# A two-layer graph network: load order, product order and sum order at the start of its first aggregation

## The chip, the cores and the metric

The kernel runs on one core of a Trainium2 chip. The metric is the device time of one execution in microseconds (us); the number quoted for a kernel is the median of its executions.

## The reference, cut to what matters

There are 16 graphs `x` of 1024 nodes with 128 features, and one adjacency matrix of 1024 x 1024 for all of them, everything in fp32.

```python
def _layernorm(x, axis=-1, eps=1e-5):
    m = jnp.mean(x, axis=axis, keepdims=True)
    v = jnp.var(x, axis=axis, keepdims=True)
    return (x - m) / jnp.sqrt(v + eps)

# layer 0
support = jnp.einsum('bnf,fo->bno', x, weight)
output = jnp.einsum('nm,bmo->bno', adj, support) + bias
x = _layernorm(x + output)

# layer 1: five steps of a gated unit
def step(h, _):
    m_in = jnp.einsum('nm,bmd->bnd', in_matrix, h)     # both matrices are adj
    m_out = jnp.einsum('nm,bmd->bnd', out_matrix, h)
    av = jnp.concatenate([m_in, m_out], axis=-1)
    u3 = h @ u3_w.T + u3_b
    z = jax.nn.sigmoid(av @ w3_w.T + w3_b + u3)
    r = jax.nn.sigmoid(av @ w4_w.T + w4_b + u3)
    hv = jnp.tanh(av @ w5_w.T + w5_b + (r * h @ u5_w.T + u5_b))
    return ((1.0 - z) * h + z * hv, None)
x = _layernorm(x + scan(step, x, length=5))
```

The costly part is adjacency times features: once per graph in layer 0, five times in layer 1. The kernel handles four graphs at a time, so there are four such aggregations in layer 0 and twenty in layer 1. The change bears on the first of these twenty-four alone.

## The kernel before

One aggregation multiplies the adjacency by the features of four graphs with Strassen's scheme (Winograd's form), on two levels. The outer level makes seven products from 2 x 2 blocks; they are done in four groups, the chains `(1, 2)`, `(3,)`, `(6, 7)` and `(5, 4)`. Within a chain, each outer product is made of seven inner ones, P1 to P7. The sums and differences of blocks that this needs run on VectorE. P1 and P2 take blocks as they are; the other five need a sum on at least one side or come later in the chain.

For the very first aggregation the adjacency has to be loaded in eight pieces (`c` = 0 to 7, 128 rows each) and turned by TensorE, and the left sums have to be made. They are then kept for all the others.

The loads and the tiles:

```python
    queues = (nc.sync, nc.scalar)

    adj_rows = adj.rearrange("(h p n c) m -> n h p c m", h=2, n=4, c=2)
    raws = [agg[:, c] if c < CH else hid[:, c - CH] for c in range(C)]   # C = 8, CH = 4
    for h in range(2):
        for c in range(h * CH, h * CH + CH):
            queues[c % 2].dma_start(raws[c], adj_rows[c // 2, c % 2])
        for k in (2 * h, 2 * h + 1):
            queues[k % 2].dma_start(rows[:, k], x_rows(k))
    # ... cut ...
    blk = [const.tile([P, 2, CH, HALF], F32, name=f"a{i}") for i in range(2)]
    # ... s1, s2, s4: [P, CH, HALF] ...
    outer = {
        1: blk[0][:, 0], 2: blk[0][:, 1], 3: s4, 4: blk[1][:, 1], 5: s1, 6: s2, 7: blk[1][:, 0],
    }
```

The left sums and the turns. `bank` gives one of three PSUM banks in turn, and the copy out of it is done by VectorE for the first half of pieces 0 to 3 and by ScalarE for the rest:

```python
    def left_sums(a11, a12, a21, a22, s1, s2, s3, s4):
        nc.vector.tensor_add(s1, a21, a22)
        nc.vector.tensor_sub(s2, s1, a11)
        nc.vector.tensor_sub(s4, a12, s2)
        return nc.vector.tensor_sub(s3, a11, a21)

    def inner_left(n):
        lt = left[n]
        left_sums(lt[1], lt[2], quarter(n, 1, 0), lt[4], lt[5], lt[6], lt[7], lt[3])
    # inner_left_12: the same for outer products 1 and 2 at once, into e12

    def turn_adj(c):
        cols = raws[c].rearrange("p (q k) -> p k q", k=C)
        i, at = divmod(c, CH)
        for j in range(2):
            pt = bank(f"pt_adj_{c}_{j}")
            pt3 = pt.rearrange("p (k q) -> p k q", k=CH)
            for k in range(CH):
                nc.tensor.transpose(pt3[:, k, :], cols[:, j * CH + k, :], ident)
            dst = blk[i][:, j, :, ts(at, P)]
            if j == 0 and i == 0:
                nc.vector.tensor_copy(dst, pt3)
            else:
                nc.scalar.copy(dst, pt3)

    for t in (pb, *seeded):            # seeding products: 12 of 128 columns
        for k in range(CH):
            nc.tensor.matmul(t[:, ts(k, P)], ident, ident, start=(k == 0), stop=True,
                             skip_group_check=True)
    for c in range(CH):
        turn_adj(c)
    last_left = inner_left_12()
```

One chain: the bank of P1 (`pa`) is copied into `pb` as the base of P6, P7 and P4, and `pc` collects P5 and P3. `hooks` names work that is put ahead of a product.

```python
    def chain(tag, src, turned, ns, results, hooks, order=(1, 5, 6, 2, 7, 3, 4)):
        # ... cut: xs, right, flat ...
        pa = ps_m.tile([P, HALF], F32, tag="a", name=f"pa_{tag}")
        pc = ps_m.tile([P, HALF], F32, tag="c", name=f"pc_{tag}")
        fa, fb, fc = flat(pa), flat(pb), flat(pc)
        x11, x12, x21, x22 = results(0, 0), results(0, 1), results(1, 0), results(1, 1)
        after = {
            1: lambda: nc.scalar.copy(fb, fa),
            5: lambda: nc.scalar.copy(x22, fc),
            6: lambda: nc.scalar.copy(x12, fb),
            2: lambda: nc.scalar.copy(x11, fa),
            7: lambda: nc.vector.tensor_add(x22, fb, x22),
            3: lambda: nc.vector.tensor_add(x12, fc, x12),
            4: lambda: nc.scalar.copy(x21, fb),
        }
        bank_of = {1: pa, 2: pa, 5: pc, 3: pc, 6: pb, 7: pb, 4: pb}
        for a in order:
            for hook in hooks.get(a, ()):
                hook()
            for o, n in enumerate(ns):
                for c in range(2):
                    product = nc.tensor.matmul(
                        bank_of[a][:, ts(o, QT)], chunk(a, o, c), left[n][a][:, c, :],
                        start=(a in (1, 5) and o == 0 and c == 0), stop=(c == 1),
                        skip_group_check=True,
                    )
            # ... cut ...
            with tc.high_priority(), behind:
                after[a]()
```

So a product is four instructions in a chain of two outer products and two in the chain `(3,)`. The first aggregation is set up like this:

```python
    def turn_rest():
        for c in range(CH, C):
            turn_adj(c)

    def outer_left():
        left_sums(outer[1], outer[2], outer[7], outer[4], s1, s2, outer[7], s4)
        inner_left(3)
    # ... in the loop over groups of four graphs ...
        if q == 0:
            hooks[12] = {
                5: [turn_rest],
                6: [outer_left, call(sums_of, rows, (3,))],
                7: [call(outer_sums, rows), call(inner_left, 6), call(inner_left, 7)],
            }
            hooks[67] = {1: [call(inner_left, 5), call(inner_left, 4)]}
            layer0_weights()
            with tc.issue_after(last_left.ins):
                sums_of(rows, (1, 2))
```

The second aggregation takes along the projections (by the layer's weight) of the first one's four graphs, with their layer normalisations. ScalarE puts the bias into a PSUM bank, TensorE adds eight products of 128 columns, VectorE adds `x` and takes the statistics, GpSimd makes scale and shift, and ScalarE applies them:

```python
    def project(q, k, y):
        # ... cut ...
        for h in range(2):
            po = seeded[h]
            with tc.high_priority():
                tc.keep_in_program_order(nc.scalar.copy(po3, b0_bc...))
            for c in range(CH):
                nc.tensor.matmul(po3[:, c, :], chunk_cols(agg[:, k], h * CH + c), w0_sb, ...)
            with tc.high_priority():
                nc.vector.tensor_add(y[:, ts(h, CH), :], po3, y[:, ts(h, CH), :])
        layernorm(y, f"0_{b}", chunked(saved[b]))

    # in layernorm
        nc.gpsimd.tensor_scalar(rstd, mv[:, :, 1], EPS, None, ALU.add)
        nc.gpsimd.tensor_tensor(rstd, rstd, power[:, :n], ALU.pow)
        nc.gpsimd.tensor_tensor(shift, mv[:, :, 0], rstd, ALU.mult)
        nc.gpsimd.tensor_scalar(shift, shift, -1.0, None, ALU.mult)
        # ... and for each of eight parts
            nc.scalar.activation(y[:, c, :], y[:, c, :], AF.Identity,
                                 bias=shift[:, c : c + 1], scale=rstd[:, c : c + 1])
```

What no call pins is put in order by the framework's scheduler when the kernel is built; after that each engine's list is fixed.

Of the kernel before, what the change touches and what calls it, by code (L numbers as in the profile page):

```python
# [10 lines left out]
F32 = mybir.dt.float32  # L11
# [9 lines left out]
def kernel(  # L21
# [99 lines left out]
    for h in range(2):  # L121
        for c in range(h * CH, h * CH + CH):
            queues[c % 2].dma_start(raws[c], adj_rows[c // 2, c % 2])
        for k in (2 * h, 2 * h + 1):
            queues[k % 2].dma_start(rows[:, k], x_rows(k))
# [28 lines left out]

    def left_sums(a11, a12, a21, a22, s1, s2, s3, s4):
        nc.vector.tensor_add(s1, a21, a22)
        nc.vector.tensor_sub(s2, s1, a11)
        nc.vector.tensor_sub(s4, a12, s2)
        return nc.vector.tensor_sub(s3, a11, a21)
# [5 lines left out]
    def inner_left_12():  # L165
        a = [[blk[0][:, :, 2 * j : 2 * j + 2, ts(i, QT)] for j in range(2)] for i in range(2)]
        return left_sums(*a[0], *a[1], e12[:, :, 0], e12[:, :, 1], e12[:, :, 3], e12[:, :, 2])

    def turn_adj(c):
        cols = raws[c].rearrange("p (q k) -> p k q", k=C)  # L170
# [4 lines that stand above are left out]
            for k in range(CH):  # L175
                nc.tensor.transpose(pt3[:, k, :], cols[:, j * CH + k, :], ident)
            dst = blk[i][:, j, :, ts(at, P)]
            if j == 0 and i == 0:
                nc.vector.tensor_copy(dst, pt3)
            else:  # L180
                nc.scalar.copy(dst, pt3)


    for t in (pb, *seeded):
        for k in range(CH):
            nc.tensor.matmul(t[:, ts(k, P)], ident, ident, start=(k == 0), stop=True,
                             skip_group_check=True)
    for c in range(CH):
        turn_adj(c)
    last_left = inner_left_12()  # L190


# [6 lines left out]
    power = const.tile([P, C], F32, name="power")  # L199
    nc.vector.memset(power, -0.5)  # L200
# [105 lines left out]
    def sums_of(src, ns, pinned=False):  # L306
        t = inner[0 if ns in ((1, 2), (6, 7)) else 1]
        for op in inner_sums(blocks_of(src, ns), [t[:, i, : len(ns)] for i in range(4)]):
            if pinned:
                tc.keep_in_program_order(op)  # L310
        return op
# [4 lines left out]
    def outer_sums(src, early=True, late=True):  # L316

        lo, hi = src[:, 0:2], src[:, 2:4]
        if early:
            nc.vector.tensor_sub(tsum[:, 2], hi[:, :, HALF:], hi[:, :, :HALF])  # L320
            nc.vector.tensor_add(tsum[:, 1], tsum[:, 2], lo[:, :, :HALF])
        if late:
            nc.vector.tensor_sub(tsum[:, 0], hi[:, :, :HALF], lo[:, :, :HALF])
            return nc.vector.tensor_sub(tsum[:, 3], lo[:, :, HALF:], tsum[:, 1])  # L324

    def chain(tag, src, turned, ns, results, hooks, order=(1, 5, 6, 2, 7, 3, 4)):
# [31 lines left out]
        bank_of = {1: pa, 2: pa, 5: pc, 3: pc, 6: pb, 7: pb, 4: pb}  # L358
        for a in order:
            for hook in hooks.get(a, ()):  # L360
                hook()
# [7 lines that stand above are left out]

                    if turned and a in (5, 6, 2) and ns in ((1, 2), (3,)) and o == c == 0:  # L370
                        tc.keep_in_program_order(product)

            behind = tc.issue_after(closed[0].ins) if closed[0] else nullcontext()
            with tc.high_priority(), behind:
                after[a]()
# [4 lines left out]
    def aggregate(tag, src, hooks, turned=True):  # L380

        c12 = agg[:, 2:4, :HALF]
# [9 lines left out]
        chain(f"12_{tag}", src, turned, (1, 2), into(first), hooks.get(12, {}))  # L392
# [6 lines left out]
        with tc.issue_after(last_outer.ins) if turned else nullcontext():  # L399
            chain(  # L400
                f"3_{tag}", src, turned, (3,), lambda i, k: agg[:, 2 + k : 3 + k, ts(i, QT)],
                hooks.get(3, {}),
# [3 lines left out]
        chain(f"67_{tag}", src, turned, (6, 7), into(src[:, 0:2]), hooks.get(67, {}))  # L406
# [5 lines left out]
            order=(1, 5, 6, 2, 7, 4, 3),  # L412
# [201 lines left out]
    def turn_rest():  # L614
        for c in range(CH, C):
            turn_adj(c)

    def outer_left():
        left_sums(outer[1], outer[2], outer[7], outer[4], s1, s2, outer[7], s4)
        inner_left(3)  # L620

    for q in range(NQ):
        room = rooms[q % 2]
        hooks = {}
        if q == 0:
            hooks[12] = {
                5: [turn_rest],
                6: [outer_left, call(sums_of, rows, (3,))],
                7: [call(outer_sums, rows), call(inner_left, 6), call(inner_left, 7)],
            }  # L630
            hooks[67] = {1: [call(inner_left, 5), call(inner_left, 4)]}
            layer0_weights()
            with tc.issue_after(last_left.ins):
                sums_of(rows, (1, 2))
# [18 lines left out]

        hooks.setdefault(67, {})["end"] = [fetch]
# [3 lines left out]
        if q == 0:  # L658
            with tc.issue_after(last_left.ins):
                aggregate(f"x{q}", room, hooks, False)  # L660
        else:
            aggregate(f"x{q}", room, hooks, False)
# [153 lines left out]
```

## Time and profile before

| What | Value |
|---|---|
| time, median of three executions | 1797.4 us |
| lowest and highest of the three | 1795.08 and 1798.0 us |
| span of the profiled execution | 1796.2 us |
| mean granted TensorE clock | 0.998 |
| TensorE busy, share of the span | 99% |
| VectorE busy | 73% |
| ScalarE busy | 44% |
| first products of the second aggregation (`pa_x<-a,hid`) | 65.34 us |

The times of single instructions are counted from the start of the span. An arrow in an instruction's name points from what it reads to what it writes: `pb<-e,inner` is a product of a left sum `e` and a right sum `inner` into the bank `pb`. `L364` is a line of the kernel. An fp32 product is recorded twice, so that `x8` in the timeline is four instructions; a turn is recorded once. What stands in brackets is the time for which the engine had been idle before, and what ended that.

### The profile page before, as it was taken

The page shows a single profiled execution, that of the slowest core. Times are in us where ns is not written, and L with a number is a line of the kernel's source. Part 1 is how long each engine was busy: PE and PEld are TensorE (multiplying, and loading weights), DVE is VectorE, ACT ScalarE, POOL GpSimd, SP SyncE. Part 2 cuts the span into 40 slices and gives each one's busy share as a digit, 9 for nine tenths or more (in the row PEclk, how much of TensorE's full clock was granted, in tenths as well). Part 3 has the DMA queues.
Part 4 walks back from the last instruction along what each step waited for, and adds up shares of the span by engine and source line. Part 5 has one row for each costly group of instructions (what it writes and reads, how often), then busy time and mean ns, then how long its engine had stood idle before and what let it go on. Part 6 is the DMA issues. An engine that isn't in the chain of part 4 may idle for free.

```text
span 1796.2 us, 19819 instructions
## 1 busy us (share of the span) xinstructions
PE 1775.3 (99%) x6709; PEld 1259.2 (70%) x6709; DVE 1309.0 (73%) x2280; ACT 789.3 (44%) x1418; POOL 94.5 (5%) x142
## 2 busy tenths in 40 slices
PE   8999999999999999999999999999999999999998
PEld 7788884857668576675857657586775857667584
DVE  7977786676857857777776857777777576867777
ACT  2345555243343434435354343534435254453536
POOL 0112220000000000000000000000000000000004
PEclk9999999999999999999999999999999999999999
DMA  6233353240513415252342414334243231513232
GB/s 225 71 118 127 109 144 74 66 95 23 117 36 90 110 36 117 60 128 59 95 103 85 105 38 115 74 85 112 58 107 105 48 81 48 118 36 94 68 74 94
DMA packets 404212, 159.23 MB, mean 89 GB/s; under 512 B 388241, under 2 KB 389137, under 8 KB 404113
## 3 DMA queue, kind: packets, MB, share of 16 engines
q1 hardware_dynamic: 403248, 154.84, 33.8%
q10 hardware_dynamic: 864, 3.15, 0.5%
q8 instruction: 53, 0.87, 0.2%
q14 instruction: 47, 0.38, 0.1%
HBM read 92.93 MB, written 65.01 MB: 88 GB/s over the span
## 4 chain that ended last, share of the span: by engine, by line
PE 89%; DVE 6%; issue 1%; DMA 1%; POOL 1%; ACT 1%; SPq 0%; DVEq 0%; POOLq 0%
PE pb L364 22%; PE pc L364 12%; PE pa L364 12%; PE pu L467 8%; PE pu L456 8%; PE seeded L472 7%; PE ph L485 7%; PE ph L484 7%; PE pc_x L364 2%; PE pa_x L364 2%; PE seeded L433 1%; POOL rstd L247 1%; DVE tsum L324 1%; DMA rows<-in_x_dram 1%; ACT ypad L252 1%
## 5 line engine op out<-in xcount | busy, mean ns | idle before, releaser
L364 PE MATMUL pb<-e,inner 128*128 128x256 f32 x864 | 206.8, 380 | 2.8 <-ACT pb L350 2.6
L364 PEld LDWEIGHTS pb<-e,inner 128*128 128x128 f32 x864 | 167.3, 194 | 23.4 <-ACT pb L350 4.7
L471 DVE TENSOR_TENSOR tsum<-tsum,hid 128x512 f32<-128x512 f32 x160 | 107.0, 684 | 96.5 <-ACT tsum L470 96.3
L501 DVE TENSOR_TENSOR tsum<-tsum,hid 128x512 f32<-128x512 f32 x158 | 108.5, 687 | 93.4 <-ACT tsum L495 93.3
L495 ACT ACTIVATE tsum<-ph,bh 128x512 f32<-128x512 f32 x158 | 108.5, 687 | 147.4 <-PE ph L485 147.3
L467 PE MATMUL pu<-agg,w_t 128*128 128x512 f32 x320 | 167.6, 610 | 0.7 <-DVE agg L416 0.7
L485 PE MATMUL ph<-tsum,u_t 128*128 128x512 f32 x320 | 163.6, 593 | 0.1
L484 PE MATMUL ph<-agg,w_t 128*128 128x512 f32 x320 | 163.7, 593 | 0.0
L472 PE MATMUL seeded<-agg,w_t 128*128 128x512 f32 x320 | 162.0, 592 | 0.0
L364 PE MATMUL pb<-s,inner 128*128 128x256 f32 x576 | 150.7, 384 | 0.5 <-DVE agg L354 0.5
L456 PE MATMUL pu<-hid,u_t 128*128 128x512 f32 x320 | 150.9, 593 | 0.0
L364 PE MATMUL pb<-a,inner 128*128 128x256 f32 x576 | 144.9, 380 | 0.7 <-DVE first L354 0.7
L364 PE MATMUL pc<-e,inner 128*128 128x256 f32 x560 | 134.6, 380 | 0.0
L470 ACT ACTIVATE tsum<-pu,br 128x512 f32<-128x512 f32 x160 | 108.7, 686 | 54.7 <-PE pu L467 47.5
L364 PEld LDWEIGHTS pb<-s,inner 128*128 128x128 f32 x576 | 109.1, 194 | 23.3 <-DVE rows L354 8.1
L364 PEld LDWEIGHTS pb<-a,inner 128*128 128x128 f32 x576 | 111.5, 195 | 15.6 <-DVE first L354 2.0
L475 ACT ACTIVATE tsum<-seeded,bz 128x512 f32<-128x512 f32 x160 | 109.2, 686 | 23.1 <-PE seeded L472 19.4
L364 PEld LDWEIGHTS pc<-e,inner 128*128 128x128 f32 x560 | 108.8, 195 | 12.7 <-issue 1.4
L503 DVE TENSOR_TENSOR hid<-hid,tsum 128x512 f32<-128x512 f32 x158 | 109.2, 691 | 10.3
L485 PEld LDWEIGHTS ph<-tsum,u_t 128*128 128x128 f32 x320 | 60.8, 190 | 76.9 <-issue 72.1
L472 PEld LDWEIGHTS seeded<-agg,w_t 128*128 128x128 f32 x320 | 60.9, 190 | 76.4 <-issue 76.4
L484 PEld LDWEIGHTS ph<-agg,w_t 128*128 128x128 f32 x320 | 60.6, 190 | 75.3 <-issue 70.4
(180 smaller groups left out, 2842.0 us busy)
## 6 DMA issues: line engine op xcount, KB each, us to landing
turned<-ypad SPq DMA_DIRECT2D x48, 512.0 KB, 3.8
rows<-turned SPq DMA_DIRECT2D x192, 128.0 KB, 2.9
hvs<-saved SPq DMA_DIRECT2D x24, 512.0 KB, 4.1
rows<-saved SPq DMA_DIRECT2D x20, 512.0 KB, 4.9
hid<-hidden SPq DMA_DIRECT2D x64, 128.0 KB, 3.6
turned<-ypad SPq DMA_DIRECT2D x32, 256.0 KB, 2.9
rows<-turned SPq DMA_DIRECT2D x128, 64.0 KB, 2.1
hid<-in_x_dram SPq DMA_DIRECT2D x12, 512.0 KB, 4.6
```

The lines of the kernel that those rows point to most:

```text
L364: product = nc.tensor.matmul(bank_of[a][:, ts(o, QT)], chunk(a, o, c), left[n][a][:, c, :], start=(a in (1, 5) and o == 0 and c == 0), sto ...
L456: pin(nc.tensor.matmul(pu, w_t["u3"], hid[:, k, ts(h, HALF)], start=True, stop=True, skip_group_check=True))
L467: pin(nc.tensor.matmul(pu, w_t["w4"], agg[:, k, cols], start=False, stop=True, skip_group_check=True))
L470: pin(nc.scalar.activation(rh[:, cols], pu, AF.Sigmoid, bias=br))
L471: pin(nc.vector.tensor_mul(rh[:, cols], rh[:, cols], hid[:, k, cols]))
L472: pin(nc.tensor.matmul(pz, w_t["w3"], agg[:, k, cols], start=False, stop=True, skip_group_check=True))
L475: pin(nc.scalar.activation(z[:, cols], pz, AF.Sigmoid, bias=bz))
L484: pin(nc.tensor.matmul(ph, w_t["w5"], agg[:, k, cols], start=True, stop=False))
L485: pin(nc.tensor.matmul(ph, w_t["u5"], rh_of[k % 2][:, cols], start=False, stop=True))
L495: pin(nc.scalar.activation(hv, ph, AF.Tanh, bias=bh))
L501: pinned(nc.vector.tensor_sub(hv, hv, hid[:, k, cols]))
L503: pinned(nc.vector.tensor_add(hid[:, k, cols], hid[:, k, cols], hv))
```

## The change

The change wants the first aggregation to start sooner and to run in a set order. It has five parts:

- The loads come in the order of need: adjacency pieces 0 and 1, the first graph (a half on each queue), pieces 2 and 3, the second graph, and then pieces 4 to 7 and the other two graphs on SyncE's queue alone. ScalarE is free of loads after its four, and a one-element copy makes it load its table early.
- P2 comes right behind P1 in this aggregation, with P1's copy into `pb` in two halves. P1 and P2 need pieces 0 and 1 and the first graph only.
- The turns of the pieces 2 and 3 are put ahead of P2 and those of 4 to 7 ahead of P5.
- VectorE's sums of this aggregation keep their program order, and the hooks spread them among the products. `outer_s3`, the last of the outer left sums, moves to the end of the first chain.
- The seeding products are three of 512 columns in place of twelve of 128.

```diff
-    for h in range(2):
-        for c in range(h * CH, h * CH + CH):
-            queues[c % 2].dma_start(raws[c], adj_rows[c // 2, c % 2])
-        for k in (2 * h, 2 * h + 1):
-            queues[k % 2].dma_start(rows[:, k], x_rows(k))
+    for queue, c in zip(queues, range(2)):
+        load_raw(queue, c)
+    for h, queue in enumerate(queues):
+        load_x(queue, 0, ts(h, HALF))
+    for queue, c in zip(queues, (2, 3)):
+        load_raw(queue, c)
+    for h, queue in enumerate(queues):
+        load_x(queue, 1, ts(h, HALF))
+    for c in range(CH, C):
+        load_raw(nc.sync, c)
+    for k in (2, 3):
+        load_x(nc.sync, k)
+    ...
+    warm = const.tile([P, 1], F32, name="warm")
+    nc.scalar.copy(warm, power[:, :1])
...
+    first_order = [True]
+    def ordered(op):
+        return tc.keep_in_program_order(op) if first_order[0] else op
     # left_sums, sums_of, outer_sums: each operation through ordered(...)
...
-            if j == 0 and i == 0:
-                nc.vector.tensor_copy(dst, pt3)
+            if j == 0 and c < 2:
+                ordered(nc.vector.tensor_copy(dst, pt3))
...
-    for c in range(CH):
+    for c in range(2):
         turn_adj(c)
-    last_left = inner_left_12()
...
+        after_next = order[1] == 2
...
+                if a == 1 and after_next:
+                    with tc.high_priority():
+                        nc.scalar.copy(fb[:, o], fa[:, o])
...
-    def aggregate(tag, src, hooks, turned=True):
+    def aggregate(tag, src, hooks, turned=True, soon=False):
+        order = (1, 2, 5, 6, 7, 3, 4) if soon else (1, 5, 6, 2, 7, 3, 4)
...
             hooks[12] = {
-                5: [turn_rest],
-                6: [outer_left, call(sums_of, rows, (3,))],
-                7: [call(outer_sums, rows), call(inner_left, 6), call(inner_left, 7)],
+                2: [call(turn_adj, 2), call(turn_adj, 3), inner_left_12],
+                5: [call(turn_adj, c) for c in range(CH, C)],
+                7: [outer_left],
+                3: [call(sums_of, rows, (3,)), call(inner_left, 3)],
+                4: [call(outer_sums, rows, True, False), call(inner_left, 6)],
+                "end": [outer_s3, call(inner_left, 7)],
             }
-            hooks[67] = {1: [call(inner_left, 5), call(inner_left, 4)]}
+            hooks[3] = {7: [call(outer_sums, rows, False), call(inner_left, 5)]}
+            hooks[67] = {1: [call(inner_left, 4)]}
             layer0_weights()
-            with tc.issue_after(last_left.ins):
-                sums_of(rows, (1, 2))
+            sums_of(rows, (1, 2))
...
+        if q == 0:
+            hooks[67][6] = [first_order.clear, call(first_order.append, False)]
...
+        aggregate(f"x{q}", room, hooks, False, q == 0)
```

In the new kernel's instruction lists, VectorE's sums do not stop at the first aggregation's end: which of the later, unpinned operations the scheduler puts where changes too, up to the layer normalisations of the first four graphs.

## The prediction

> **What bounds the kernel now.** First I read the page's busy times and its chain that ended last:
>
> ```profile
> PE 1775.3 (99%) x6709; PEld 1259.2 (70%) x6709; DVE 1309.0 (73%) x2280; ACT 789.3 (44%) x1418; POOL 94.5 (5%) x142
> ...
> PE 89%; DVE 6%; issue 1%; DMA 1%; POOL 1%; ACT 1%; SPq 0%; DVEq 0%; POOLq 0%
> ```
>
> TensorE is the bound of the whole, so only time in which it waits can be won. The listings of the instructions of both kernels, engine by engine, agree in all but numbering from the second aggregation's layer normalisations on (about 110 us). So I read only the first 100 us. Each engine works through its list in order, so in what follows I walk the new lists with the old durations. The busy times by stretches of 10 us (PE, PEld, DVE, ACT, POOL, clock, DMA share, GB/s):
>
> ```profile
> 10.00:20.00 10.00, 8.44 (x59) 7.89 (x60) 7.12 (x9) 6.96 (x14) 0.00 (x0) 1.00 0.98 365
> 20.00:30.00 10.00, 10.00 (x47) 8.50 (x45) 10.00 (x10) 2.34 (x4) 0.00 (x0) 1.00 0.73 227
> 30.00:40.00 10.00, 8.10 (x33) 5.52 (x32) 10.00 (x14) 1.84 (x5) 0.00 (x0) 1.00 0.31 124
> 40.00:50.00 10.00, 8.36 (x37) 6.61 (x36) 10.00 (x17) 2.17 (x4) 0.00 (x0) 1.00 0.01 2
> ...
> 80.00:90.00 10.00, 7.37 (x39) 6.04 (x38) 8.59 (x36) 4.92 (x12) 5.26 (x6) 0.96 0.29 105
> 90.00:100.00 10.00, 10.00 (x49) 9.04 (x49) 6.71 (x25) 5.76 (x16) 2.72 (x5) 0.87 0.25 94
> ```
>
> TensorE misses 1.6, 1.9 and 1.6 us in three of the first stretches and 2.6 us at 80 to 90. The chain over the first 120 us says who holds it:
>
> ```profile
> 14.23 1.22 DVE e L156
> ...
> 21.27 2.20 DVE s L156
> ...
> 45.10 0.61 DVE inner L291
> 45.72 0.04 issue
> 45.76 1.99 PE pc_x L364 x8
> ```
>
> From 14.2 to 45.7 us the end is set by VectorE, which never rests; from 45.76 by the products. In the timeline, the last hole is this:
>
> ```profile
> 87.44 0.49 ACT L252 ACTIVATE ypad<-ypad,shift,rstd 128x128 f32<-128x128 f32 x1 [2.87 <-POOL shift L249]
> 87.84 0.36 ACT L350 COPY pb<-pa_x 128x256 f32<-128x256 f32 x1
> 88.26 1.20 PE L364 MATMUL pb<-e,inner 128*128 128x256 f32 x4 [2.58 <-ACT pb L350]
> ```
>
> A normalising activation waits for GpSimd's shift, the copy into pb stands behind it on ScalarE, and TensorE waits for the copy.
>
> [...] starts lie 0.60 and 2.20 us apart, and 1.13 for 1024, 0.34 for 256. I use these. [...] 410 GB/s at 10 to 11 us with both queues, and 410 at 31 to 32 us with SyncE's alone. Putting the late adjacency rows on one queue should cost nothing. [...]
>
> **Loads.** Each 0.5 MB takes 1.26 us at 415 GB/s. In the old order the sixth (x1) landed near 11.5, which gives landing near 3.6 + 1.26k us. Reordered: adjacency c0 and c1 by 6.1, x0 at 7.4, c2 and c3 at 9.9, x1 at 11.2, c7 at 16.2. x0 comes 4 us sooner; the last needed pieces come as before, since the rate is full throughout. Three seeding products of 512 columns replace twelve of 128: the same columns, hidden behind the first load. The early table load takes 1.3 us off ScalarE at 8.8, before anything waited for it long.
>
> **Turns, P1 and P2.** One tile's four turns cost 0.5 us (1.51 for twelve), one product instruction 0.43 us (1.73 for four). TensorE's order now is: four tiles of c0 and c1, the first tile of c2, half of P1, the second of c2, half of P1, c3, then all of P2, then c4 to c7. c2 is there at 9.9, so: 10.4, P1 half to 11.3, 11.8, 12.7, c3 to 13.7, P2 to 15.4. ScalarE copies P2's bank at 15.5 to 16.1, before the eight tiles of c4 to c7, which take 0.52 us each (4.15 for eight): done at 20.3. Before, this group ran 15.39 to 19.54. So P2 (1.7 us of TensorE) is pulled forward, and the second half of the adjacency is complete 0.8 us later. P5 starts near 19.7 and not 18.67.
>
> **VectorE's fixed order.** The inner sums of x0 and x1 go first, 11.25 to 13.65 (4 x 0.60). The four e sums wait for ScalarE's last copy of c3 (14.4): 14.45 to 19.0. Then it waits for c7 until 20.35. Up to the sum that releases P5 of the chain (6,7) follow: three of 2048 elements, one more of 2048 (2.20 each), five of 1024 (1.13: four outer sums, and the sum of first into agg, formerly behind this point), fifteen of 512 (0.60: two evacuations, twelve left sums, this sum), six of 256 (0.34). That is 8.8 + 5.65 + 9.0 + 2.04 = 25.5, so it ends at 45.9, where the old one ended at 45.7. What the early start wins (2.4 us of inner sums before 13.65) is spent on a 1.35 us wait, 1.13 for the agg sum, and 0.2 of later e sums.
>
> **The rest of the first aggregation.** Products left at that point: the old kernel has 44 instructions, as P1 of both parts of (5,4) is done; the new one 46, as only half of that P1 is ahead. Its P4 and the second half of the next P1 change places too. With 46 + 4 instructions before the next P5: 46.0 + 50 x 0.432 + about 0.5 of bank waits = 68.1, against 67.2 by the same counting before. That is 0.9 us **later**.
>
> **The projections after it.** VectorE's new order has two short sums and one of 1024 elements ahead of the first projection's additions, and these now start after P4's copy at 67.9: 6 x 0.60 + 2 x 0.34 + 1.13 gives 73.4, against 69.76. Behind the statistics stand another 1024 sum and the second projection's addition, so the first mean and variance are complete at 78.3 (before 74.4), GpSimd's four steps end at 81.4 and the six activations at 83.8. The third projection's products start at 84.4 and not 80.50; TensorE waits some 3 us. Against that, the second image's statistics no longer stand behind the third projection's additions: complete at 83.4, shift at 86.5 (before 87.41). The copy into pb comes at 89.6 after only a trace of waiting, where the old kernel lost 2.58. By the second half of P2 of that chain both stand at 93.5; if the 3 us hole halves the clock as the old one did, the new one is 1.2 later.
>
> **Sum.** The first aggregation +0.9, the projections -0.9 to +0.3: between 0 and +1.2 us. Nothing after that has a time of its own to keep, so it stays.
>
> **Rivals.** One: the early start carries through. If P2 does not delay the c4 copies (ScalarE idle enough, c7 done at 18.5), VectorE never waits, P5 of (6,7) starts at 44.2, and by the same walk the projections meet less waiting: -3.5 us, 1794. For it speaks that VectorE alone sets 14 to 46 us, and idles before 14; against it the order of ScalarE's copies. Two: the hole of 2.58 us vanishes and no new one opens, because the statistics come sooner than I place them: -2 to -3 us, 1795. For it: the second image's chain is clearly freed. Against: the first one's is clearly later. Three: the new hole halves the clock and delays twice: +3, 1800.5. The trace already shows one such slow stretch after 2.6 us. A fourth, that one queue or 2 KB rows of x starve the turns, I hold for small: c7 has 2 us of slack at TensorE.
>
> **Range and chances.** The walk alone gives 1797.4 to 1798.6. The first two rivals together are as likely as the third and larger, so I put the middle at 1797.0 us. The rivals reach from -3.5 to +3, and three timings of before differ by 2.9 us, so the range is 1793.0 to 1801.0. All TensorE waiting before 100 us is about 10 us, 0.6%, so 2% either way needs an accident: faster 0.005, same 0.985, slower 0.01.
>
> **What would show it.** Right: P1 begins near 10.5 and P2 ends near 15.4; the c4 to c7 copies end near 20.3 and VectorE waits for them; P5 of (6,7) near 46; the first projection's addition near 73; a TensorE wait of about 3 us before the third projection, and next to none before the pb copy. Wrong: a VectorE with no wait at 19 to 20 us, P5 of (6,7) before 45, or a change after 110 us that is not a mere shift.

## The result, and the profile after

| | before | after |
|---|---|---|
| time, median | 1797.61 us | 1803.32 us |
| lowest and highest | 1795.08 to 1798.16 us | 1801.78 to 1805.74 us |
| span of the profiled execution | 1796.2 us | 1800.6 us |

The ratio of after to before is 1.0036, with a 95% interval of 1.0023 to 1.0049. The change makes the kernel some 5.7 us slower; predicted was 1797.0 us (1793.0 to 1801.0).

The page of after, busy times and shares of the chain that ended last:

```profile
PE 1774.5 (99%) x6691; PEld 1256.4 (70%) x6691; DVE 1309.0 (73%) x2278; ACT 791.6 (44%) x1424; POOL 94.6 (5%) x142
...
PE 87%; DVE 6%; DMA 2%; ACT 2%; issue 2%; POOL 1%; SPq 1%; DVEq 0%; ACTq 0%; POOLq 0%
```

TensorE has 18 records fewer (nine fp32 products at two records each), and as many weight loads fewer. TensorE's share of the chain is down from 89% to 87%, that of DMA up from 1% to 2%: something now waits for a transfer.

The first 100 us of after in stretches of 10 us (PE, PEld, DVE, ACT, POOL, clock, DMA share, GB/s):

```profile
10.00:20.00 10.00, 9.99 (x68) 9.28 (x68) 7.31 (x8) 7.39 (x15) 0.00 (x0) 1.00 0.96 367
20.00:30.00 10.00, 9.21 (x42) 7.32 (x40) 9.82 (x9) 1.25 (x4) 0.00 (x0) 1.00 0.94 318
30.00:40.00 10.00, 6.58 (x28) 5.17 (x29) 9.75 (x16) 2.79 (x7) 0.00 (x0) 1.00 0.10 34
40.00:50.00 10.00, 8.80 (x32) 6.77 (x33) 10.00 (x15) 1.53 (x3) 0.00 (x0) 0.83 0.00 0
...
80.00:90.00 10.00, 8.32 (x46) 6.91 (x44) 8.14 (x35) 6.68 (x16) 3.84 (x8) 1.00 0.22 81
90.00:100.00 10.00, 10.00 (x55) 8.89 (x54) 8.15 (x26) 6.83 (x18) 6.39 (x7) 1.00 0.34 121
```

TensorE is fuller from 10 to 20 us (P2 is pulled forward) and emptier from 30 to 40. The hole at 80 to 90 is 1.7 us and not 2.6, and the slow clock has moved from 80 to 100 us to 40 to 50. The timeline of after at the old hole:

```profile
84.06 2.15 PE L466 MATMUL seeded<-w_sb,agg 128*128 128x128 f32 x16 [1.68 <-ACT seeded L463]
...
88.81 0.37 ACT L376 COPY pb<-pa_x 128x256 f32<-128x256 f32 x1
...
89.23 1.13 PE L391 MATMUL pb<-e,inner 128*128 128x256 f32 x4
```

The copy into `pb` no longer waits, and the hole stands before the third projection. By the end of this chain's P2, near 93 us, after is 0.5 us **ahead** of before. So the loss lies later. The same table in stretches of 20 us, for before:

```profile
100.00:120.00 20.00, 20.00 (x93) 17.29 (x92) 14.24 (x24) 9.08 (x20) 1.35 (x3) 1.00 0.39 138
...
160.00:180.00 20.00, 20.00 (x100) 17.30 (x99) 17.12 (x28) 5.68 (x10) 0.00 (x0) 1.00 0.44 136
```

and for after:

```profile
100.00:120.00 20.00, 17.33 (x81) 14.95 (x79) 10.78 (x15) 8.53 (x19) 0.25 (x1) 1.00 0.41 136
...
160.00:180.00 20.00, 17.85 (x83) 15.30 (x81) 14.06 (x20) 5.31 (x11) 0.00 (x0) 1.00 0.33 106
```

After loses 2.67 us in the first and 2.15 us in the second. The stretch between them (120 to 140 us) differs by 0.12 us, and from 200 to 1700 us the busy times agree within 0.3 us. With the lead of 0.5 us this is the whole: 2.67 + 2.15 + 0.12 - 0.5 = 4.4 us, the difference of the two spans. (The medians are 5.7 us apart; the six executions of each kernel scatter by 3 to 4 us, and one of each was profiled.)

The chain of after through the first of the two holes (start in us, us, what):

```profile
101.50 0.50 ACT rows L278
102.02 4.68 DMA saved<-rows
...
106.72 0.33 SPq L108
...
107.10 5.25 DMA saved<-rows
112.37 3.64 DMA rows<-in_x_dram
...
116.10 1.23 DVE tsum L346
...
119.47 0.61 DVE hid L380
...
120.12 0.70 PE pb L391 x2
```

The reader is to see a relay. `rows` held the first four graphs. When the layer normalisation of the third of them is done, SyncE issues its store to `saved` (102.02). Only when that has landed may the buffer be loaded again (106.72), and SyncE's queue stands at that load, so the fourth graph's store is issued after it (107.10), while it is under way. The load behind that store lands at 116.0. VectorE's sum of the new graph waits for it, a product's bank waits for VectorE, and TensorE idles 2.8 us. In before the two stores take 2.63 and 3.54 us (102.56 to 105.19, 106.54 to 110.08):

```profile
102.56 0.33 SPq L258 DMA_DIRECT2D saved<-rows  x1
105.19 0.33 SPq L108 DMA_DIRECT2D rows<-in_x_dram  x1
```

The waits of that sum on its loads, in before between 95 and 200 us (the last three numbers are us in total, times, longest):

```profile
DVE tsum L320 <- DMA hid<-in_x_dram: 1.2, 1, 1.2
DVE tsum L320 <- DMA rows<-in_x_dram: 1.1, 1, 1.1
```

and in after:

```profile
DVE tsum L346 <- DMA rows<-in_x_dram: 4.0, 1, 4.0
DVE tsum L346 <- DMA hid<-in_x_dram: 3.4, 1, 3.4
```

The first is the relay at 100 to 120 us, the second the same relay at 156 to 175 us, where the second group's graphs leave the other buffer, `hid`, and the fourth group's are loaded into it. Of the 4.0 us, 1.2 are hidden behind TensorE's work; the rest is the hole of 2.8.

**Why a store of the same 512 KB takes 4.68 us and not 2.63** is told by the transfers. This is the view of DMA of after from 102 to 107 us: 40 slices of 0.125 us, busy share in tenths and rate, and the queues:

```profile
DMA  0000005699997999600020001000000000000000
GB/s 0 0 0 0 0 0 229 262 557 393 393 426 295 459 393 393 262 0 0 0 33 0 0 0 33 0 33 33 33 0 33 33 33 0 0 0 0 0 0 0
...
q1 hardware_dynamic: 144, 0.52, 26.5%
q8 instruction: 1, 0.02, 2.0%
```

The store's bulk runs at about 400 GB/s and is over by 104.2 us. Then single pieces trickle at 33 GB/s until 106.1. In the packet records, these are the last eight of the store's packets of 4096 bytes from 104.58 to 106.22 us, mostly 159 ns each, and each begins as the one before it ends, as if a single engine still had work. The records name no engine, but the one packet of the queue `instruction` in this view (16,384 bytes, begun at 103.03, 1565 ns) ends at 104.59, just where the eight begin, so I take it for what held this engine up. The store ends with sixteen packets of 4 bytes: fifteen have come by 104.3 us, the sixteenth comes at 106.22, and the load behind the store is issued at 106.72, 0.5 us after that one. In before the sixteen of the same store come from 104.66 to 104.82 us, and the load is issued at 105.19, 0.4 us after the last.

### The profile page after: what moved, and what is told of

Read it like the earlier page. It is cut to its first block, busy times and chain, and to the rows that moved or that the text cites. A ratio compares the mean times of both kernels' runs of the same rounds, so it can differ in the third digit from the quotient of the medians.

```text
span 1800.6 us, 19796 instructions
## 1 busy us (share of the span) xinstructions
PE 1774.5 (99%) x6691; PEld 1256.4 (70%) x6691; DVE 1309.0 (73%) x2278; ACT 791.6 (44%) x1424; POOL 94.6 (5%) x142
## 4 chain that ended last, share of the span: by engine, by line
PE 87%; DVE 6%; DMA 2%; ACT 2%; issue 2%; POOL 1%; SPq 1%; DVEq 0%; ACTq 0%; POOLq 0%
PE pb L391 21%; PE pc L391 12%; PE pa L391 12%; PE pu L500 8%; PE seeded L505 7%; PE pu L489 7%; PE ph L518 7%; PE ph L517 7%; PE pa_x L391 2%; PE pc_x L391 1%; PE seeded L466 1%; POOL rstd L273 1%; DMA saved<-rows 1%; DVE tsum L535 1%; DVE ypad L558 1%
## 5 line engine op out<-in xcount | busy, mean ns | idle before, releaser
L391 PEld LDWEIGHTS pb<-a,inner 128*128 128x128 f32 x576 | 111.6, 195 | 15.4 <-issue 1.9
```

The lines of the kernel that those rows point to most:

```text
L391: product = nc.tensor.matmul(bank_of[a][:, ts(o, QT)], chunk(a, o, c), left[n][a][:, c, :], start=(a in (1, 5) and o == 0 and c == 0), sto ...
```

## The experiments

**Theory A, the fetch**, supposes that the packets of 16,384 bytes on the queue that the profile names `instruction` bring in an engine's instruction list while the kernel runs; no record says what they hold, and I call each a fetch. There are 53 of them on q8 in the trace of after; TensorE's 13,382 records (products and weight loads) over 53 are 252 per packet, so I take them for TensorE's list. With nine products fewer at the start, the list is 36 records shorter, each later packet would come at a later point of the work, and two of them now fall on the two stores (begun at 103.03 and 157.5 us). Then it is the **seeding products**, the part of the change that seemed to matter least, that costs the time. **Theory B:** the new order of the loads costs it. **Theory C:** the new order of P2, turns and sums does.

Each ratio below is to executions of before that were timed along with the run (medians 1798.41 us for e1 to e4, 1798.39 for e5 to e8, 1798.0 for e9 to e11). Four medians lie outside the range that was stated for them, by 0.03 to 0.13 us (e1, e2, e5, e7), which is less than the scatter; e3 is a clear miss.

Both directions first, e1 (all of the change but the seeding products) and e2 (these alone).

```diff
 # e1: after, with the twelve products again; e2: the reverse, in before
-        nc.tensor.matmul(t (all 512 columns), ident, ident[:, None, :].broadcast_to([P, CH, P]), ...)
+        for k in range(CH):
+            nc.tensor.matmul(t[:, ts(k, P)], ident, ident, start=(k == 0), ...)
```

> The changed kernel with the twelve seeding products of 128 columns put back; all else as changed. Theory A (fetch): the loss comes from TensorE's instruction fetch (16 KB packets of the instruction queue), which in the changed kernel falls at 103.0 us into the store of the third normalised graph and delays one DMA engine's share of it; nine fp32 products are 36 instructions, some 3.7 us of TensorE's list, so the fetch moves to about 99.5 us, the store lands in 2.6 us and not 4.7, VectorE's wait for rows at the first outer sum falls from 4.0 to about 1 us, TensorE is full from 100 to 120 us, and the time is 1797 us (1795.5 to 1798.5). Theory B (the new load order and its semaphores make the stores late) and theory C (the new order of VectorE's sums does): the seeding products are hidden before the first load, so the time stays at 1803 (1801.5 to 1805).

> The kernel before with only the three seeding products of 512 columns in place of the twelve. Theory A (fetch): the fetch moves from 100.5 to about 104 us, into the store that runs from 102.6 to 105.2; the store lands 1 to 2 us later, and the time rises to 1799 to 1803 us. If the fetch just misses the store's packets, the time stays, and only the trace can tell. Theories B and C: 1797.5 us, no change, since neither loads nor sums are touched.

Measured: e1 1798.63 us (1796.97 to 1800.43), ratio to before 1.0004 [0.9996, 1.0013]; e2 1803.12 us (1799.7 to 1804.78), 1.0025 [1.0015, 1.0034]. So the seeding products alone make the loss, and all the rest of the change together makes no difference that can be measured. The stores of e1, as SyncE issued them and the loads behind them:

```profile
103.22 0.33 SPq L282 DMA_DIRECT2D saved<-rows  x1
105.85 0.33 SPq L108 DMA_DIRECT2D rows<-in_x_dram  x1
107.20 0.33 SPq L282 DMA_DIRECT2D saved<-rows  x1
110.69 0.33 SPq L108 DMA_DIRECT2D rows<-in_x_dram  x1
```

The first store takes 2.63 us again (105.85 - 103.22), and the DMA view of e1 from 103 to 108 us has no instruction packet and no trickle:

```profile
DMA  0000000089899898995000000000009194336657
...
q1 hardware_dynamic: 201, 0.76, 46.3%
```

TensorE's stretches at 100 and 160 us are full (20.00 each), although e1 is 1.2 us behind after at the first store: its clock was 0.68 from 40 to 50 us, and after's 0.83. So the fetch and the store came apart from both sides, the fetch earlier by 1.37 us (101.66 and 103.03) and the store later by 1.20. e8, further down, has e1's TensorE list up to there without the slow stretch: its store is 0.7 us earlier (102.53), its fetch 0.8 (100.87). Between these two traces the clock moves both, and the lead of the fetch stays, 1.56 us in e1 and 1.66 in e8.

In e2, the fetch did not come near 104, as was expected, but at 108.05, and it is the second store that is hit:

```profile
106.12 0.33 SPq L260 DMA_DIRECT2D saved<-rows  x1
111.06 0.33 SPq L108 DMA_DIRECT2D rows<-in_x_dram  x1
```

4.94 us (3.54 for this store in before, where the load ahead of it is under way as well). That the time came near the expected range is in part luck, as the place was another. TensorE loses 0.92 us in the first stretch and 2.34 us (also a clock of 0.91) in the second, where the fetch at 155.9 falls on the store issued at 155.22.

**e3: another number of products**, more instead of fewer: each of the twelve split in two of 64 columns.

```diff
-        for k in range(CH):
+        for k in range(2 * CH):
-            nc.tensor.matmul(t[:, ts(k, P)], ident, ident, ...)
+            nc.tensor.matmul(t[:, ts(k, P // 2)], ident, ident[:, ts(k % 2, P // 2)], ...)
```

> The changed kernel with twenty-four seeding products of 64 columns. Theory A (fetch): 84 instructions more than the changed kernel, so the fetch comes at about 94.5 us, clear of the third and fourth graph's stores (102 to 110 us); it may meet the second graph's store at 94.4, whose load nobody needs soon. Time 1797 us (1795.5 to 1799.5). Theories B and C: 1803 us, or more if the seeding runs past the first load.

Measured: 1802.44 us (1801.39 to 1803.61), 1.0023 [1.0014, 1.0033]. A miss in the time, and the fault of the experiment. The stores are clean (2.63 us, fetch 4.9 us ahead of the first) and TensorE's two stretches nearly full (20.00, 19.80), but the timeline of the start shows

```profile
4.81 7.03 PE L213 MATMUL seeded<-ident 128*128 128x64 f32 x32
11.64 4.32 PE L203 MATMUL pt_adj<-ident,agg 128*128 128x128 f32 x20
```

that the seeding now lasts until 11.84 us: the turns begin at 11.64 and not 6.02, and the first store is issued at 107.31, 4.1 us later than in e1. The fetch was expected at 94.5 and came at 102.4, as all of the work came later. The run shows a store that no fetch hits and no loss behind it; for the time it decides nothing, as the late start alone costs about as much as the two holes.

**e7: six products of 256 columns**, between the two, in after.

```diff
+        for k in range(2):
+            nc.tensor.matmul(t (256 columns, half k), ident, ident[:, None, :].broadcast_to([P, 2, P]), ...)
```

> The changed kernel with six seeding products of 256 columns: twelve instructions more than the changed kernel, twenty-four fewer than with twelve products. Theory A (fetch): against the issue of the third graph's store the fetch came 1.0 us late in the changed kernel and 1.5 us early with twelve products, so here some 0.2 us late, just as the store's packets begin; the store is held up by part of the fetch, lands in 3 to 4.5 us, and the time lies between: 1799 to 1802.5 us. If it were not the instruction count but the 512-column products themselves, the time would be that of twelve, 1798.5.

Measured: 1802.6 us (1800.03 to 1807.47), 1.0023 [1.0016, 1.0031]. The fetch at 104.0 (1641 ns) falls on the first store (issued at 103.27, 4.49 us); that at 155.6 is over before the store at 157.83 (2.63 us). TensorE shows the first hole (1.43 us short from 100 to 120 us, and 1.06 us shorter than before from 120 to 140) and not the second (20.00). Yet the median is as high as with two holes. The stretches of 100 us show one more place, in which e1 and after are full: from 1200 to 1300 us, 99.05 us busy. There the chain of e7 has

```profile
1234.82 5.05 DMA turned<-ypad
```

a transfer that takes features out and back for turning, with a fetch at 1237.4 us in its middle. The load behind it is issued after 5.12 us, and in before, e1 and after, where no fetch falls on it, after 3.89 us each. The sum that waits for it waits 1.5 us, and TensorE 0.95. So this pair of stores is not the only sensitive place.

**e4 and e8: SyncE's queue.** The four stores of the two relays (the third and fourth graph of the first and of the second group; the expectations of e4 and e9 name other groups) go out by ScalarE's queue, which has just finished the normalisation, so that a late store holds up no other graph's store or load: e4 in after, e8 in e1.

```diff
-            nc.sync.dma_start(store, y)
+            (nc.scalar if tag in ("0_2", "0_3", "0_6", "0_7") else nc.sync).dma_start(store, y)
```

> The changed kernel with the stores of the third and fourth normalised graph issued by ScalarE in the first three groups, so that the fourth's store no longer stands on SyncE behind a load that waits for the third's. Theory A (fetch): the fetch still falls at 103 us and the third graph's store still takes over 4 us, but the fourth's is issued near 106.0 and not 107.1 and lands near 109; its load is issued near 109.5 and not 112.4, VectorE's wait falls below 1.5 us, and the time is 1798.5 us (1797 to 1800.5). If the stores' delay comes from the load order (B) in another way than through SyncE's queue, or from the sums (C), the time stays at 1803.

> Twelve seeding products and the stores on ScalarE's queue together, on the changed kernel. Theory A (fetch): the fetch misses the stores already, so taking the queue's blocking away wins only part of VectorE's 1.2 us of waiting, which TensorE did not feel: 1798 us (1796 to 1799.5), the same as twelve products alone. If the stores' queue costs something of its own, apart from the fetch: 1796 or less.

Measured: e4 1799.31 us (1796.95 to 1803.04), 1.0009 [1.0000, 1.0017]; e8 1797.6 us (1797.14 to 1800.01), 0.9996 [0.9988, 1.0005]. In e4 a fetch still falls on the first store of either relay (103.11 us, 1593 ns, and 154.78; the loads behind these stores are issued 4.73 and 4.47 us after them). But the fourth graph's store goes out at 106.53, ahead of the load at 106.89 and not behind it, and its own load at 109.83, where after has 112.37. The sum's two waits are only 1.3 and 2.4 us (the second more than the 1.5 expected) and TensorE's stretches 20.00 and 19.20. Two things qualify this. The trace is of the fastest of e4's executions (1796.95 us). And in this kernel the scheduler put one more product instruction (0.43 us) ahead of the one that waits, at both places, as in e8 to e10; up to 0.43 us of each hole is closed by that. With the stores' other queue, and this, the loss against before falls from 0.36% to 0.09%. Where no fetch hits (e8), the other queue changes little against e1.

**e5 and e6: the loads alone, and the orders alone**, both with twelve seeding products. e5 is before with the new block of loads (without the early copy that moves ScalarE's table load of 1.28 us from 8.83 us in before to 3.56 in after; the expectation counts it in), e6 is e1 with the old block (the early table copy stays).

> The kernel before with the new load order alone (its early table load with it); twelve seeding products, old product and sum order. Theory A (fetch): TensorE's list is the same, so the fetch stays near 100.5 us and the stores near 102.6, apart; no loss of 5 us. What is left is what the loads are worth: P1 no longer waits for x0 until 11.5, pieces 2 and 3 come 1.2 us later, the first e sum starts near 13.8 and not 14.23: time 1798 us (1796.5 to 1800). Theory B (the load order makes the stores late): 1803.

> The changed kernel with twelve seeding products and the old load order; product and sum order as changed. Theory A (fetch): the fetch is at 101.7 or a little later and the stores move later with the first aggregation, so no collision; P1 and P2 wait for x0 until 11.5, P2 ends near 16.5, the turns of the last four pieces and VectorE's first outer sum come about 1 us later than in the changed kernel: 1799.5 us (1798 to 1801.5). Theory B: as the changed loads are gone, the loss should be gone whatever the seeding; it cannot be told from A here, but with the run before this one it can. Theory C (the sum order costs the 5 us): 1803.

Measured: e5 1796.47 us (1794.31 to 1799.44), 0.9990 [0.9982, 0.9998]; e6 1800.62 us (1797.62 to 1804.17), 1.0013 [1.0004, 1.0021]. The loads win about 1.9 us, the orders with the old loads cost about 2.2 us, and the sum agrees with e1's 0.2. The first store says the same: at 101.75 in e5, 102.56 in before, 103.22 in e1 and 106.56 us in e6, where the set order meets late data (the first product at 12.10 and not 10.15 us). B falls as a cause of the loss; C costs something, but it isn't what makes after slow. In neither kernel does a fetch fall on a store.

**e9: the cure in the kernel where the seeding products alone are changed** (e2 with the stores on ScalarE's queue, the edit of e4), and **e10: the same in e5**, as the best candidate.

> The kernel before with the three wide seeding products and, besides, the four stores of the first and third group issued from ScalarE's queue. Theory A (an instruction fetch holds up one engine's share of a store; SyncE's queue in order then carries the delay to the loads behind it): the store may still land late, but the last two loads no longer stand behind a store's issue, so the waits of the sum of the graphs on its load fall from 2.1 and 3.5 us to at most 1.5 and 2.5, and the time goes from 1803.1 to 1798.5 to 1800. Theory B (the order of the first loads) and C (the order of sums and turns) say nothing of it, as neither is in this kernel: they leave 1803.

> The kernel before with the new order of the first loads, twelve seeding products and the four stores on ScalarE's queue. Theory A: the fetches come before the stores anyway, at about 100 and 152 us, so the stores' other queue wins only what is left of the wait for loads (1.7 us at one place): 1795 to 1797, at or below the 1796.5 of the same kernel with its stores on SyncE's queue. A rival, that ScalarE pays for the issues: 1798 to 1800.

Measured: e9 1799.5 us (1796.46 to 1802.73), 1.0005 [0.9997, 1.0013]; e10 1796.4 us (1794.34 to 1800.1), 0.9992 [0.9986, 0.9999]. The time of e9 is as expected, one of its waits isn't: 2.7 and 1.5 us, where at most 1.5 and 2.5 were to come. Its chain:

```profile
107.81 4.92 DMA saved<-rows
...
112.79 3.47 DMA rows<-in_x_dram
```

The fetch at 109.7 falls on the fourth graph's store, and that graph's own load has to wait for it on any queue. (A second fetch, at 158.14, falls on the store of 156.78, which takes 4.53 us.) The other queue cures the relay between graphs, not the late store itself. In e10 the fetches stay clear, and the queue adds nothing to e5 that can be told apart. e5 and e10 are below both kernels, by about 0.1% of before.

**e11: the count of instructions, and nothing else of the seeding.** After keeps its three wide products; eighteen turns of the identity that nothing reads are added, which run between 26.0 and 33.3 us, in part in TensorE's gaps, one record and one weight load each: 36 again. (For it, the scheduler also moved one instruction of a P1 from 33 to 36 us, behind six others.)

```diff
+    def idle_turns(n):
+        pt3 = bank(f"pt_idle_{n}").rearrange("p (k q) -> p k q", k=CH)
+        for k in range(n):
+            nc.tensor.transpose(pt3[:, k % CH, :], ident, ident)
...
-            hooks[3] = {7: [...]}
-            hooks[67] = {1: [call(inner_left, 4)]}
+            hooks[3] = {2: [call(idle_turns, 8)], 7: [...]}
+            hooks[67] = {1: [call(inner_left, 4), call(idle_turns, 10)]}
```

> The changed kernel with its three wide seeding products, and with eighteen turns of the identity, which nothing reads, in TensorE's gaps between 26 and 41 us: 36 more TensorE instructions ahead of 100 us, as many as the nine products that the change took away, but in another place and of another kind. Theory A: the fetch comes before the store again (by about 1.5 us, and not 1.0 after its issue), both stores land in about 2.6 us, TensorE's stretches at 100 to 120 and 160 to 180 us are full but for 0.3, and the time falls from 1803.3 to 1798 to 1800. If the seeding products mattered for their own time or shape at the start, or the orders of sums and loads for the loss: 1803 or, with the turns' 2.3 us in the way, up to 1805.

Measured: 1799.64 us (1797.72 to 1800.65), 1.0005 [0.9997, 1.0014]: with some 2.5 us of useless work **added** (0.71 + 1.15 + 0.60 us in the timeline), the kernel is faster than after, whose ratio is 1.0036 [1.0023, 1.0049], and the medians differ by 3.7 us. The stores of the first relay:

```profile
103.12 0.33 SPq L284 DMA_DIRECT2D saved<-rows  x1
105.75 0.33 SPq L108 DMA_DIRECT2D rows<-in_x_dram  x1
107.10 0.33 SPq L284 DMA_DIRECT2D saved<-rows  x1
110.70 0.33 SPq L108 DMA_DIRECT2D rows<-in_x_dram  x1
```

and TensorE's two stretches:

```profile
100.00:120.00 20.00, 19.88 (x93) 17.15 (x92) 13.04 (x21) 9.64 (x22) 1.26 (x3) 1.00 0.46 154
...
160.00:180.00 20.00, 19.93 (x99) 17.20 (x98) 16.58 (x24) 5.68 (x10) 0.00 (x0) 1.00 0.41 137
```

The fetch comes at 101.3, 1.8 us ahead of the store, the store takes 2.63 us, and the holes are gone. So the three wide products do not cost the time by their own length or width. What removes the loss is 36 more TensorE instructions ahead of the store. (e11's clock was as slow as e1's from 40 to 47 us, so its store is 1.1 us later than after's; but its fetch is 1.76 us earlier.)

All kernels whose stores go by SyncE's queue alone, side by side: the fetch that lies next to the first store of each relay (from the packet records) and what that store took until the load behind it was issued:

| kernel | first relay: store issued, fetch, store took | second relay: store issued, fetch, store took |
|---|---|---|
| before | 102.56, 100.5, 2.63 us | 154.70, 153.0, 2.63 us |
| **after** | 102.02, **103.0, 4.70** | 156.89, **157.5, 4.10** |
| e1 | 103.22, 101.7, 2.63 | 155.41, 153.2, 2.64 |
| e2 | 106.12 (second store), **108.0, 4.94** | 155.22, **155.9, 4.42** |
| e3 | 107.31, 102.4, 2.63 | 159.50, 150.8, 2.63 |
| e5 | 101.75, 99.9, 2.63 | 153.93, 151.6, 2.65 |
| e6 | 106.56, 104.2, 2.62 | 158.73, 156.5, 2.62 |
| e7 | 103.27, **104.0, 4.49** | 157.83, 155.6, 2.63 |
| e11 | 103.12, 101.3, 2.63 | 155.32, 153.4, 2.64 |

Where a fetch began in the 2 us after a store's issue, the store took over 4 us (five cases, bold; e2's first one is a second store, which takes 3.54 us in before); where it began at least 1.5 us ahead, 2.62 to 2.65 us. The stores on ScalarE's queue that a fetch met in the same way, two each in e4 and e9, took 4.47 to 4.98 us. Each row is one profiled execution.

## Why the prediction was wrong

**The walk through the first 95 us held in most places.** Predicted and measured: P1's first half from 10.4, measured 10.31 us; P2's end 15.4 and 15.53; the c4 to c7 copies' end 20.3 and 20.07; P5 of (6,7) 46.0 and 46.62; the first projection's addition 73.4 and 72.23; the third projection's products 84.4 and 84.06; the copy into `pb` 89.6 and 88.81, with P6 behind it at 89.23 without a wait; the end of P2 93.5 and 93.0. Sizes were off: VectorE's inner sums began at 12.31 and not 11.25, as they waited for the second graph (the rule for the loads, 3.6 + 1.26k, puts it at 11.2, and already falls short of the 11.5 that was read for it in before), so that its wait for c7 was 0.39 and not 1.35 us; and the hole before the third projection was 1.68 and not 3 us and didn't slow the clock, which was 1.00 from 80 to 100 us. The first part of the sum, "between 0 and +1.2 us", was measured at -0.5, and that it came so near is in part luck: the next aggregation's P5 began at 68.99 (before 67.06), so the first aggregation cost 1.9 and not 0.9 us, some of it by products at half clock behind a hole of 1.76 us at 40 us (four instructions of `pa_x` took 1.81 us at 40.02 and 1.03 us at 43.95), which the walk did not have; and the projections won 2.5 us, where 0.9 was the most expected. The two belong together: the third projection began when its chain of VectorE, GpSimd and ScalarE let it, as foretold, and a TensorE that came later waited less for it.

**The step that failed** is the last: "Nothing after that has a time of its own to keep, so it stays." From about 110 us on the instruction lists agree, but agreeing lists do not make equal times: packets of q8 (which I take to bring in TensorE's list) fell on the stores at 102 and 157 us, and these took 4.70 and 4.10 us and not 2.63. So the stores did have a time to keep: they had to stay clear of these packets. The term left out is +4.9 us (2.67 + 2.15 + 0.12), four times the largest that I had for the first 100 us. The decision before it, "So I read only the first 100 us", kept the relay of stores and loads out of sight; its slack stood in the trace of before, in the sum's waits of 1.1 and 1.2 us that TensorE did not yet feel, and so did the fetch at 100.5, two microseconds ahead of the store.

**The part that was dismissed was the one that counted.** "The same columns, hidden behind the first load" is right for the time of the seeding products (the turns behind them begin at 6.38 us in after and 6.02 in e1, and wait for a load later on in both) and wrong for their number.

**The rivals** all lay in the first 100 us. The third came nearest in its figure (1800.5), but by a slow clock behind the new hole at 84 us, and there the clock stayed at 1.00; none of the three had a transfer late in it. That a hole slows the clock was read from one case, 0.87 from 90 to 100 us behind the 2.58 us in before; the cases of both traces stand at the end. The text's own sign for a failure, "a change after 110 us that is not a mere shift", is what showed.

**The range** was drawn from the rivals' reach and the scatter of three timings. It held no room for a term outside the stretch that was read.

**What stays open:** that the packets of q8 carry TensorE's list is inferred; no record names the engine. Their number fits, they shift with TensorE's instructions alone (e2, e11), and they follow TensorE's count: from one packet to the next after's TensorE starts 248 records in the mean, with a scatter (standard deviation) of 14%, while VectorE's count scatters by 40% and the time by 27%. In all thirteen traces the fourth packet comes when TensorE has started 899 to 947 records, although the time is 99.9 to 109.7 us. But the exact place does not follow from the count: with 36 records fewer ahead, the fourth packet came 24 records later in the rest of the list from e1 to after, and 74 from before to e2. So the count foretells that a fetch moves, and not which store it hits; for that the trace is needed.

## What to carry to other kernels

In this kernel a change in the number of instructions at the start moved the later instruction packets against the work (the one nearest the first store from 101.66 us in e1 to 103.03 in after, and to 101.3 in e11), and cost microseconds where nothing was edited (1803.32 us in after, 1798.63 in e1, 1799.64 in e11): look at the instruction queue beside each store or load on which something waits with little slack. Before calling the rest of a list "a mere shift", look in the trace of before for hand-overs that are nearly late; here these were two waits of 1 us at a sum. Where a store may come late, it should not stand in one queue in order with the loads of other buffers: with the stores on ScalarE's queue, the loss of 0.36% in the changed kernel fell to 0.09%, and that of 0.25% in e2 to 0.05%. Where no fetch met a store, the other queue won nothing clear (e8, e10).

## What the runs showed of the hardware

- An instruction packet of 16,384 bytes took 0.88 to 1.87 us in after, a data packet of 4096 bytes 0.16 us. Behind a transfer that met one, the next load was issued later by 1.2 to 2.1 us (5.12 us after the issue and not 3.89 at `turned<-ypad`, e7; 4.70 and not 2.63 at the first store, after). In after that load was issued at 106.72, behind the last of the store's sixteen packets of 4 bytes (106.22), and not behind the fifteenth (104.26).
- At the start of the run a product of 64 columns took as long as one of 128: twenty-four of 64 columns took 10.5 us in e3 (1.34 to 11.84), twelve of 128 columns 4.8 us in e1 (1.34 to 6.18): 0.44 and 0.40 us each. The runs do not show why.
- TensorE's clock records have two values in the traces of before and after, full and one half. Up to 1775 us each trace has one stretch of half clock, 3.41 us long: in before from 89.19 us, behind the hole of 2.58 us that ended at 88.26, and in after from 40.27, behind the hole of 1.76 us that ended at 40.02. Behind the hole of 1.68 us that ended at 84.06 in after the clock stayed at 1.00. In the 3.41 us ahead of the two stretches TensorE was busy for 0.93 and 1.38 us; from 81.23 to 84.64 in after, for 1.73 us. e1 and e8 have the same TensorE list up to the first store, and the mean clock was 0.68 from 40 to 50 us in e1 and 1.00 over the first 100 us in e8, so the list alone did not decide. What does, the runs do not show.
